# A four-layer graph network on one core: the edge sums' weighting moved to ScalarE, the last router moved into the join, and three sets of transfers moved to GpSimd's queue

## The chip, the cores and the metric

The kernel runs on one core of a Trainium2 chip. The core has five engines, each with its own queue of instructions that it takes in order: TensorE (PE, with its weight loads, PEld), VectorE (DVE), ScalarE (ACT), GpSimd (POOL) and SyncE (SP). SP, ACT and POOL also issue transfers (DMAs); a transfer stands in the queue of the engine that issues it, so an issue that has to wait holds whatever stands behind it. The metric is the time of one execution on the device, in microseconds (us). Lower is better.

## The reference

3125 nodes with 256 features each go through four layers. Each layer adds a graph part (gnn) and a mixing part (mix) computed from the normalized features, and then a feed-forward part (ffn):

```python
xn = _layernorm(x, axis=-1)
x = x + _L3_gnn_ref(xn, edge_index, ...) + _L3_mix_ref(xn[None], ...)[0]
x = x + _L3_ffn_ref(_layernorm(x, axis=-1)[None], ...)[0]
```

The graph parts of layers 1, 2 and 3 are attention over edges: for every head, an edge from s to t gets `exp(leaky_relu(s_src[s] + s_tgt[t]))`, these are normalized over the edges that end in t, and the projected features of s are summed with them. Layers 1 and 2 have two such steps each (several heads, then one head of 256), layer 3 one, which it joins with a sequence part through a gate. The ffn of layers 1 and 3 sends tokens to 8 experts. Layer 1 uses the two best experts of a token and a shared one; layer 3 the best one, with places for 489 tokens per expert:

```python
probs = jax.nn.softmax(x @ gate_w + gate_b, axis=-1)
idx = jnp.argmax(probs, axis=-1)
pos = (jnp.cumsum(one_hot, axis=0) * one_hot).sum(-1).astype(jnp.int32) - 1
kept = pos < C
buf = jnp.zeros((E, C, D)).at[idx, pos_safe].set(x, mode='drop')
hmid = jax.nn.relu(jnp.einsum('ecd,edf->ecf', buf, w1) + b1[:, None, :])
ybuf = jnp.einsum('ecf,efd->ecd', hmid, w2) + b2[:, None, :]
y_tok = ybuf[idx, pos_g] * (prb * kept)[:, None]
```

## The kernel before

The nodes lie in 25 tiles of 125 (NT, P), held in SBUF as X. Stages that go tile by tile take them in seven groups of four tiles (GROUPS, the last has one). The layers follow each other: layer 0 to about 1497 us of the span, layer 1 to 3400, layer 2 to 4660, layer 3 to the end. The code is written in a framework that orders the instructions of each engine itself, within the blocks between branches, by an estimate of when each could run; so steps of neighbouring program parts interleave, and the order on an engine is fixed at build time. An instruction waits for semaphores of the engines and transfers that it depends on, also for the memory of a pool that is reused.

**Edge sums.** `gat_products` (L1168) sums over edges as dense products. For each head the exponential of the leaky sum is split in a factor of the source (`gpre`, L1180), one of the target (`mine`) and a maximum. `h` holds the projected features of all tiles with a column of ones. It is multiplied by `gpre` in place, tile by tile (L1187 to L1189), every third tile on POOL, the others on DVE. Then, for five groups of five target tiles, the factors of the targets are spread into rows (PE product L189, copied by ACT and DVE in turn, L78 and L80), and for each of the 25 source tiles s an adjacency block `a` is loaded by SP, DVE makes the weights t from it (L1232), and PE adds t times h (L1237). With narrow heads `sums_by_feature` (L1252) does the same the other way round, for four columns of 7, 6, 6 and 6 target tiles, with t on DVE in L1308 and the products in L1313 and L1322. The function is used five times: layer 1's four heads of 128 (from 1657 us) and one of 256 (2332), layer 2's four of 64 (3630) and one of 256 (4160), and layer 3's four of 64 (5522). `shares` (L1336) and `elu` (L1383) finish each target tile through the function `use` that the caller gives.

**Second weights.** `gat_heads` (L1392) loads W2 and forms its products with the two attention vectors (`folded`, L973 and L974 on DVE) after the first projection of the layer is done, in its own pool.

**Layer 1's experts.** In `l1_ffn` 50 scatters on POOL's queue (`scatter`, L2272) write every token twice into rows in DRAM, sorted by expert; the last four columns of a row tell which token it is and its weights. These columns are loaded back as `ends` (L1580) by ACT's queue, in two halves of 112 and 13 partitions (L886 and L887 in `halves`). Ten steps on DVE (L1585 to L1594) make from them where each result goes. Meanwhile PE runs the shared expert group by group: eight hidden blocks, each with its gelu on ACT (L605), then four output tiles that DVE adds to X (L1604). The results wait in PSUM banks of a pool of seven. In DVE's order the ten steps stand after the additions of the first group and ahead of all others.

**Layer 3.** The normalized features are in DRAM. `l3_gnn` loads them as `local` on ACT's queue (L2319). `l3_local` (L2012) adds the bias to them on POOL (L2037) and runs the edge sums; its `use` adds the sums to `local` and takes the elu. `l3_join` (L2430) gathers the sequence part's rows (`gather`, L2268), normalizes both, computes a gate and a feed-forward part, adds the result z to X on POOL (L2500), normalizes X into `wide` and turns it into XNT for PE. `l3_ffn` (L2520) then fills two DRAM buffers with zeros (buf, where the experts' tokens go, and ybuf, where the results go; L2540 and L2543, by SP and ACT in turn), computes the router's logits for all tiles on PE, the softmax, each token's rank over experts, its position, and its place `put` (L2586), sends 25 scatters on POOL's queue to buf, and runs the experts one after the other: SP loads weights and rows `xr` (L2606), PE turns the rows, hidden, output; the results are scattered to ybuf.

Of the kernel before, what the change touches and what calls it, by code (L numbers as in the profile page):

```python
# [11 lines left out]
F32 = mybir.dt.float32  # L12
# [48 lines left out]
class Net:  # L61
# [1106 lines left out]
    def gat_products(self, far, h, al, heads, width, loops, use):  # L1168
# [3 lines left out]
        with ExitStack() as es:  # L1172
# [14 lines left out]
            for s in range(NT):  # L1187
                eng = nc.gpsimd if s % 3 == 2 else nc.vector
                eng.tensor_mul(h[:, s], h[:, s], pre[:, s, :, None].to_broadcast([P, heads, width + 1]))  # L1189
            if width < 96:  # L1190
                self.sums_by_feature(es, mine, over, h, heads, width, loops, use)
                return
# [20 lines left out]
            for g in range(NG):  # L1213
# [10 lines left out]
                for s in range(NT):  # L1224
                    a = ap.tile([P, GW], F32, name="a")
                    self.load_edges(a, self.adj_rows(), s, g)
                    if loops and s // GB == g:
                        blk = a[:, (s % GB) * P:(s % GB + 1) * P]
                        nc.vector.tensor_add(blk, blk, self.ident[:P, :P])
                    t = tp.tile([P, heads, GW], F32, name="t")  # L1230
# [21 lines left out]
    def sums_by_feature(self, es, mine, over, h, heads, width, loops, use):  # L1252
# [35 lines left out]
        for i0, n in COLUMNS:  # L1288
# [10 lines left out]
            for s in range(NT):  # L1299
                a = ap.tile([P, most], F32, name="a")  # L1300
                self.halves(nc.sync, a[:, :w], self.adj_rows()[s * P:(s + 1) * P, i0 * P:i0 * P + w])
                if loops and i0 <= s < i0 + n:
                    blk = a[:, (s - i0) * P:(s - i0 + 1) * P]
                    nc.vector.tensor_add(blk, blk, self.ident[:P, :P])
                t = []
# [86 lines left out]
    def gat_heads(self, prefix, h, al, h2, al2, heads, width, loops, eps):  # L1392
# [4 lines left out]
        h2v = h2[:, :, 0, :D]  # L1397
        with ExitStack() as es:
            wp = es.enter_context(self.pool("tg_w"))
            kp = es.enter_context(self.pool("tg_k", 2))  # L1400
            w2 = wp.tile([128, chunks, D + 2], F32, name="w2a")
            nc.sync.dma_start(w2[:, :, :D], self.ins[prefix + "W2"].rearrange("(c p) m -> p c m", p=128))
            b1 = self.rows(wp, prefix + "b1")
            with self.pool("tg_f") as fp:
                self.folded(fp, w2[:, :, :D], chunks, 1, [prefix + "a_src2", prefix + "a_dst2"],
                            w2[:, :, D:])
# [125 lines left out]
    def l1_ffn(self, given):  # L1532
# [8 lines left out]
        with ExitStack() as es:  # L1541
# [10 lines left out]
            with ExitStack() as es2:  # L1552
# [27 lines left out]
                self.halves(nc.scalar, ends, rows[:, D:].rearrange("(q p) c -> p q c", p=P))  # L1580
# [154 lines left out]
    def layer1(self):  # L1735
# [4 lines left out]
        with self.pool("g1_h2") as low:  # L1740
            last = self.last_terms(low)
            with self.pool("g1_h") as hp:
                with self.pool("in1") as ip:
# [3 lines left out]
                self.gat_heads(pre, h, al, *last, 4, 128, False, 1e-16)  # L1747
# [189 lines left out]
    def layer2(self):  # L1937
        pre = "L2_gnn_"
        with self.pool("g2_h2") as low:
            last = self.last_terms(low)  # L1940
            with self.pool("g2_h") as hp:
                with self.pool("in2") as ip:
# [3 lines left out]
                self.gat_heads(pre, h, al, *last, 4, 64, True, 0.0)  # L1946
# [68 lines left out]
    def l3_local(self, out, h, al, far, flag, most, found):  # L2015
# [4 lines left out]
        with ExitStack() as es:  # L2020
# [16 lines left out]
            nc.gpsimd.tensor_add(out, out, gb[:, None, :].to_broadcast([P, NT, D]))  # L2037

            def use(pp, i, acc, eps):
                x = kp.tile([P, D], F32, name="agg")  # L2040
                self.shares(kp, x, acc, 4, 64, less[:, i, :] if eps is None else eps)
                nc.vector.tensor_add(out[:, i, :], out[:, i, :], x)
# [232 lines left out]
    def l3_gnn(self):  # L2275
# [5 lines left out]
        with self.pool("in3_k") as keep:  # L2281
# [32 lines left out]
            with self.pool("in3_t") as tp:  # L2314
                xnt = tp.tile([128, KC, N], F32, name="XNT")
                wide = h.rearrange("p i h c -> p i (h c)")
                with self.pool("g3_h") as hp:
                    local = hp.tile([P, NT, D], F32, name="local")
                    self.halves(nc.scalar, local, rows.rearrange(by_tile, p=P))  # L2319
                    self.l3_local(local, h, al, *found)  # L2320
                    lp = over.enter_context(self.pool("out_ps", 3, PSUM))
                    self.l3_join(rows, local, self.order, ys, wide, xnt, lp)
                self.l3_ffn(wide, xnt, lp)
# [106 lines left out]
    def l3_join(self, rows, local, rank, ys, wide, xnt, lp):  # L2430
# [5 lines left out]
        with ExitStack() as es:  # L2436
# [6 lines left out]
            b2, fg = (self.rows(sp, pre + k) for k in ("ff2_b", "ln2_g"))  # L2443

# [64 lines left out]
            gated(*GROUPS[0], *turned[0])  # L2509
            for k, group in enumerate(GROUPS):  # L2510
                if k + 2 <= last:
                    got[k + 2] = fetched(*GROUPS[k + 2])
                if k + 1 <= last:
                    gated(*GROUPS[k + 1], *turned[k + 1])
                joined(*group, turned[k][0])
                if k + 2 <= last:
                    turned[k + 2] = halves_of(*GROUPS[k + 2], *got[k + 2])

    def l3_ffn(self, wide, xnt, lp):


# [191 lines left out]
```

## Time and profile before

| what | us |
|---|---|
| median of 3 runs | 6647.1 (6640.66 to 6662.06) |
| the profiled execution | 6652.58 |
| its span in the trace | 6650.5 |
| PE busy in it | 5730.2 |
| layer 3 from the first edge-sum product to the first expert | 5531 to 6368 |

The profiled execution's mean granted clock of TensorE is 0.911 of full speed. A row of the timeline gives the start in us from the span's start, the duration, the engine, the line of the code, the operation, output and inputs with shapes, and how many such instructions are taken together (x17). Brackets at its end give how long the engine had been idle before and what it was released by; ACTq and SPq are the queues that issue transfers. In a table of groups the columns are busy time, mean duration of one in ns, and idle time before it. Idle time of an engine matters where another engine waits for it.

### The profile page before, as it was taken

Reading aid. Unit: us, or ns where it says so; the run is one execution under the profiler, and the core shown is the slowest. Engines: PE = TensorE matmul, PEld = TensorE weight load, DVE = VectorE, ACT = ScalarE, POOL = GpSimd, SP = SyncE. Lnnn points to the kernel's source line nnn. Section 1 sums busy time; section 2 is a strip of 40 time slices with the busy share of each in tenths; the row PEclk is TensorE's granted clock in tenths of the full one; section 3 lists DMA queues with packets and bytes.
Section 4 is the critical chain, followed back from the end, with each engine's and each line's share of the span. In section 5 each row is a group of like instructions: output and inputs, shape, how many; then the busy total and the mean of one; then the engine's idle time right before and its main releaser. Section 6 shows DMA issues by size and latency. Waiting matters only on the chain. (4 is left out here: it accounts for less than half of the span.)

```text
span 6650.5 us, 80016 instructions
## 1 busy us (share of the span) xinstructions
PE 5730.2 (86%) x30063; PEld 3902.5 (59%) x30063; DVE 3734.0 (56%) x7804; ACT 1695.3 (25%) x3532; POOL 917.8 (14%) x714
## 2 busy tenths in 40 slices
PE   5887999996999998699976999999878887997876
PEld 4555975664899877468853344776534443333644
DVE  7734333128877644115036887546378888886433
ACT  2433432331011100113333011002256560003411
POOL 0000100004000012301111000120334552002021
PEclk7888999997999999789987999999889998998888
DMA  2644668101222143215520222430332223222132
GB/s 80 106 64 67 181 197 244 31 5 68 62 63 63 45 140 111 66 51 168 173 88 20 83 81 61 138 112 1 88 46 57 57 50 94 71 77 69 46 120 94
DMA packets 436886, 571.69 MB, mean 86 GB/s; under 512 B 130447, under 2 KB 321372, under 8 KB 432687
## 3 DMA queue, kind: packets, MB, share of 16 engines
q1 hardware_dynamic: 363116, 468.81, 26.4%
q10 hardware_dynamic: 44907, 68.00, 3.7%
q0 software_dynamic: 28416, 29.15, 1.6%
q8 instruction: 252, 4.13, 0.3%
q14 instruction: 195, 1.59, 0.1%
HBM read 450.03 MB, written 115.55 MB: 85 GB/s over the span
## 5 line engine op out<-in xcount | busy, mean ns | idle before, releaser
L1232 DVE SCALAR_TENSOR_TENSOR t<-rows,over,a 125x625 f32<-125x625 f32 x750 | 619.6, 866 | 426.3 <-PE acc L1237 418.9
L1308 DVE SCALAR_TENSOR_TENSOR t<-rows,over,a 125x750 f32<-125x750 f32 (+1 forms) x800 | 793.3, 1045 | 75.4 <-PE acc L1322 70.6
L1313 PE MATMUL acc<-t,g_h 125*64 125x375 f32 (+1 forms) x3200 | 596.5, 500 | 12.2 <-DVE t L1308 12.2
L1237 PE MATMUL acc<-g_h,t 125*125 125x129 f32 x5000 | 574.5, 274 | 6.2 <-ACT x L1363 3.5
L1237 PE MATMUL acc<-h,t 125*125 125x257 f32 x2500 | 558.4, 383 | 19.8 <-DVE t L1232 10.0
L1237 PEld LDWEIGHTS acc<-g_h,t 125*125 125x125 f32 x5000 | 566.2, 188 | 10.8 <-ACT x L1363 4.2
L1237 PEld LDWEIGHTS acc<-h,t 125*125 125x125 f32 x2500 | 467.3, 189 | 103.9 <-PE acc L1237 18.8
L1313 PEld LDWEIGHTS acc<-t,g_h 125*64 125x64 f32 x3200 | 220.0, 136 | 340.1 <-issue 238.8
L1322 PE MATMUL acc<-t,g_h 125*32 125x375 f32 (+1 forms) x3200 | 359.1, 496 | 0.0
L2215 POOL TENSOR_TENSOR bx<-h,crow 128x500 f32<-128x500 f32 (+1 forms) x224 | 263.7, 1195 | 308.9 <-issue 79.3
L2221 PE MATMUL y<-bx,ident 128*128 128x500 f32 (+1 forms) x448 | 222.7, 611 | 66.0 <-POOL bx L2215 64.3
L931 DVE SCALAR_TENSOR_TENSOR X<-ps_out,prob,X 125x256 f32<-125x256 f32 x200 | 87.9, 479 | 338.7 <-PE ps_out L181 338.5
L2212 DVE TENSOR_TENSOR_SCAN h<-da,state,bx 128x500 f32<-128x500 f32 (+1 forms) x224 | 246.2, 1130 | 18.3 <-ACT da L2210 15.8
L605 ACT ACTIVATE h<-ps_hidden,L_ffn_b,bn_s 128x500 f32<-128x500 f32 (+1 forms) x224 | 160.4, 723 | 350.9 <-PE ps_hidden L181 330.1
L1322 PEld LDWEIGHTS acc<-t,g_h 125*32 125x32 f32 x3200 | 99.6, 109 | 236.3 <-issue 235.5
L181 PE MATMUL ps_hidden<-xbt,w 128*128 128x250 f32 x928 | 206.2, 380 | 22.3 <-ACT xbt L166 21.9
L864 PE MATMUL agg<-h,few 125*125 125x257 bf16 x1875 | 212.6, 274 | 4.3 <-ACT few L861 2.2
L864 PEld LDWEIGHTS <-few 125*125 125x125 bf16 x1875 | 207.9, 137 | 6.1 <-ACT few L861 3.3
L181 PE MATMUL ps_out<-w,hb 128*125 128x256 f32 x928 | 205.0, 379 | 0.0
L181 PEld LDWEIGHTS ps_hidden<-xbt,w 128*128 128x128 f32 x928 | 175.1, 191 | 49.0 <-ACT xbt L166 28.6
L181 PE MATMUL ps_hidden<-XNT,L_ffn_W 128*128 128x500 f32 (+1 forms) x448 | 195.8, 562 | 0.0
L181 PEld LDWEIGHTS ps_out<-w,hb 128*125 128x125 f32 x928 | 174.0, 188 | 25.9
(765 smaller groups left out, 9461.0 us busy)
## 6 DMA issues: line engine op xcount, KB each, us to landing
a<-adj SPq DMA_DIRECT2D x500, 273.4 KB
a<-adj SPq DMA_DIRECT2D x150, 328.1 KB
arow<-adj SPq DMA_DIRECT2D x25, 1367.2 KB
adj<-block SPq DMA_DIRECT2D x22, 1531.2 KB
w<-in_L_ffn_W1p SPq DMA_DIRECT2D x29, 1024.0 KB
w<-in_L_ffn_W2p SPq DMA_DIRECT2D x29, 1024.0 KB
crow<-crows ACTq DMA_DIRECT2D x96, 250.0 KB
a<-adj SPq DMA_DIRECT2D x50, 382.8 KB
```

Of the source, the lines that this page charges most:

```text
L181: self.nc.tensor.matmul(ps, lhsT[k], rhs[k], start=(k == 0), stop=(k == n - 1))
L605: self.nc.scalar.activation(out[:, f, :], ps[:, :nt], func, **kw)
L864: nc.tensor.matmul(acc[b][:P, :D + 1], few[:, b * P:(b + 1) * P], h[k][:, s, :], start=(s == 0 and k == 0), stop=(s == NT - 1 and k == 2))
L931: nc.vector.scalar_tensor_tensor(x, ps, prob[:, g + j, e:e + 1], x, op0=ALU.mult, op1=ALU.add)
L1232: nc.vector.scalar_tensor_tensor(t[:, hd, :], rows[:, hd, :], over[:, s, hd:hd + 1], a, op0=ALU.max, op1=ALU.mult)
L1237: nc.tensor.matmul(acc(b, hd), t[:, hd, b * P:(b + 1) * P], h[:, s, hd, :], start=(s == 0 and first), stop=(s == NT - 1), skip_group_check ...
L1308: nc.vector.scalar_tensor_tensor(t[hd][:, :w], rows[hd][:, :w], over[:, s, hd:hd + 1], a[:, :w], op0=ALU.max, op1=ALU.mult)
L1313: nc.tensor.matmul(acc[k][c][q * width:(q + 1) * width, :c1 - c0], h[:, s, 2 * k + q, :width], t[2 * k + q][:, c0:c1], start=(s == 0), sto ...
L1322: nc.tensor.matmul(acc[pairs][c][hd * 32:(hd + 1) * 32, :c1 - c0], h[:, s1, hd, width:].to_broadcast([P, 32]), t1[hd][:, c0:c1], start=(s1 ...
L2212: nc.vector.tensor_tensor_scan(h[:, :w], da[:, :w], bx[:, :w], state[:, c, s:s + 1], op0=ALU.mult, op1=ALU.add)
L2215: nc.gpsimd.tensor_mul(bx[:, :w], h[:, :w], crow[:, :w])
L2221: nc.tensor.matmul(acc[c][:, :w], self.ident, terms[c][:, :w], start=(s == 0), stop=(s == S - 1))
```

## The change

1. **Weighting.** The loop over all tiles ahead of the edge sums is gone. A function `weigh(s)` multiplies one tile by its factors on ACT, one instruction per head, and is called for each source tile in the first group (or first column).
2. **Second weights.** A new function `last_weights` loads W2 and folds it; layers 1 and 2 call it before the layer's input is formed.
3. **Layer 1's columns.** `ends` is loaded by POOL's queue.
4. **Layer 3's local part.** `local` is loaded by POOL's queue. The bias is added to each tile's sums on DVE in `use`, no longer to all of `local` on POOL.
5. **Zeros.** A new function `l3_buffers` fills buf and ybuf by POOL's queue, in 8 and 7 transfers, before `l3_local`.
6. **Router.** A new function `l3_router` is set up in `l3_join`. Logits of a group are computed in the join one group later. Positions are settled in two stretches, tiles 0 to 15 and 16 to 24, each with its own softmax and with counts carried over in `before`; the choice is made by the largest probability and the first expert among equals, without ranks. The first stretch's steps are written into the join after its fifth group, the second's after its end; each sends its scatters.

```diff
-            for s in range(NT):
-                eng = nc.gpsimd if s % 3 == 2 else nc.vector
-                eng.tensor_mul(h[:, s], h[:, s], pre[:, s, :, None].to_broadcast([P, heads, width + 1]))
+            def weigh(s):
+                for hd in range(heads):
+                    nc.scalar.activation(h[:, s, hd, :], h[:, s, hd, :], AF.Copy, scale=pre[:, s, hd:hd + 1])
...
+                    if g == 0:
+                        weigh(s)
                     t = tp.tile([P, heads, GW], F32, name="t")
...
+                if i0 == 0:
+                    weigh(s)
                 t = []
...
+    def last_weights(self, pool, prefix, wide):
+        chunks = wide // 128
+        w2 = pool.tile([128, chunks, D + 2], F32, name="w2a")
+        self.nc.sync.dma_start(w2[:, :, :D], self.ins[prefix + "W2"].rearrange("(c p) m -> p c m", p=128))
+        b1 = self.rows(pool, prefix + "b1")
+        with self.pool("tg_f") as fp:
+            self.folded(fp, w2[:, :, :D], chunks, 1, [prefix + "a_src2", prefix + "a_dst2"], w2[:, :, D:])
+        return w2, b1
...
-                self.halves(nc.scalar, ends, rows[:, D:].rearrange("(q p) c -> p q c", p=P))
+                self.halves(nc.gpsimd, ends, rows[:, D:].rearrange("(q p) c -> p q c", p=P))
...
             with self.pool("g1_h") as hp:
+                weights = self.last_weights(hp, pre, 512)
                 with self.pool("in1") as ip:
...
-            nc.gpsimd.tensor_add(out, out, gb[:, None, :].to_broadcast([P, NT, D]))
-
             def use(pp, i, acc, eps):
                 x = kp.tile([P, D], F32, name="agg")
                 self.shares(kp, x, acc, 4, 64, less[:, i, :] if eps is None else eps)
+                nc.vector.tensor_add(x, x, gb)
                 nc.vector.tensor_add(out[:, i, :], out[:, i, :], x)
...
-                    self.halves(nc.scalar, local, rows.rearrange(by_tile, p=P))
+                    self.halves(nc.gpsimd, local, rows.rearrange(by_tile, p=P))
+                    buf, ybuf = self.l3_buffers(hp)
...
+            most = GROUPS[4][0]
+            sent = settle(0, most)
             for k, group in enumerate(GROUPS):
...
+                if k:
+                    logits(*GROUPS[k - 1])
+                if k > 4:
+                    next(sent, None)
                 joined(*group, turned[k][0])
+                if k == 4:
+                    next(sent)
...
+            logits(*GROUPS[last])
+            self.through(settle(most, NT))
...
+    def l3_buffers(self, pool):
+        zero = pool.tile([P, 4 * (D + 2)], F32, name="zero")
+        nc.vector.memset(zero, 0.0)
+        zv = buf[:32 * P, :].rearrange("(b p r) d -> b p (r d)", b=8, p=P)
+        for b in range(8):
+            nc.gpsimd.dma_start(zv[b], zero)
...
+        def logits(g, n):
+            ps = lp.tile([128, 512], F32, name="ps_router", tag="mm")
+            for j in range(n):
+                self.product(ps[:P, j * 8:(j + 1) * 8],
...
+        def settle(t0, t1):
...
+            nc.vector.tensor_sub(p, p, each(m))
+            nc.scalar.activation(p, p, AF.Exp)
...
+            yield
...
+            for i in range(n):
+                nc.vector.tensor_copy(off[:, i, :], before)
+                nc.vector.tensor_add(before, before, ps[:P, 256 + i * 8:256 + (i + 1) * 8])
...
+            for i in range(t0, t1):
+                stores.append(self.scatter(buf, put[:, i:i + 1], wide[:, i, :D + 2]))
```

## The prediction

> **What bounds it now.** I read the page first, then the waits of TensorE (PE), then the timeline around each edit.
>
> ```profile
> PE 5730.2 (86%) x30063; PEld 3902.5 (59%) x30063; DVE 3734.0 (56%) x7804; ACT 1695.3 (25%) x3532; POOL 917.8 (14%) x714
> ```
>
> PE is busy for 5730 of 6650.5 us, so the kernel is a row of PE stages with some 920 us of gaps, and an edit is worth the gap that it closes. Most edits aim at one. The first is the start of an edge-sum stage:
>
> ```profile
> 1657.58 17.19 DVE L1189 TENSOR_TENSOR g_h<-g_h,gpre 125x516 f32<-125x516 f32 x17 [0.79 <-ACT gpre L1180]
> ...
> 1675.16 0.99 PE L189 MATMUL ps_spread<-ident,mine 125*125 125x125 f32 x3 [14.94 <-DVE rows L78]
> ```
>
> A bracket gives the idle time before an instruction and what ended it. Seventeen multiplications fill VectorE (DVE) and PE's copies queue behind them: 14.94 us of nothing on PE. The second gap is in layer 1's expert stage, where ScalarE's (ACT) queue holds a load that waits for the scatters:
>
> ```profile
> 2772.18 3.71 ACTq L887 DMA_DIRECT2D ends<-f_rows  x1
> ...
> 2776.67 13.34 PE L181 MATMUL ps_out<-w,hs 128*125 128x256 f32 x52 [49.86 <-ACT hs L605]
> ...
> 2778.63 0.27 DVE L1585 TENSOR_TENSOR other<-ends,number 125x64 f32<-125x64 f32 x1 [67.03 <-DMA ends<-f_rows]
> ```
>
> Two engines stand there: PE 49.86 us for ACT, and DVE 67.03 us for the columns. The third is the start of layer 3's edge sums, with three gaps in a row (ACT's queue, DVE's weighting, GpSimd's weighting behind its addition):
>
> ```profile
> 5510.70 10.18 ACTq L887 DMA_DIRECT2D local<-xn  x1
> ...
> 5522.19 5.86 DVE L1189 TENSOR_TENSOR g_h<-g_h,gpre 125x260 f32<-125x260 f32 x17 [9.87 <-ACT gpre L1180]
> ...
> 5534.40 13.67 POOL L2037 TENSOR_TENSOR local<-local,L_gnn_gat_b 125x6400 f32<-125x6400 f32 x1 [30.70 <-SPq L2709]
> ...
> 5549.05 3.87 PE L1313 MATMUL acc<-t,g_h 125*64 125x500 f32 x8 [11.13 <-DVE t L1308]
> ```
>
> The last is the way from layer 3's join to its first expert:
>
> ```profile
> 6275.39 16.96 PE L181 MATMUL ps_router<-L_ffn_gate_w,XNT 128*125 128x8 f32 x80 [0.52 <-DVE z L2497]
> ...
> 6282.09 0.72 POOL L2500 TENSOR_TENSOR X<-X,z 125x256 f32<-125x256 f32 x1 [7.61 <-DVE z L2499]
> 6320.67 1.23 POOL L2272 DMA_INDIRECT buf<-g_h,put  x1 [37.86 <-DVE put L2586]
> ...
> 6356.57 1.19 POOL L2272 DMA_INDIRECT buf<-g_h,put  x1 [0.30 <-issue]
> ...
> 6368.11 2.81 PE L181 MATMUL ps_hidden<-xt,L_ffn_w 128*128 128x489 f32 x3 [0.51 <-ACT xt L80]
> ```
>
> 25 scatters at 1.494 us each, all after the last router step, all on the chain of waits.
>
> **Weighting in the first group (four places).** 17 multiplications on DVE and 8 on GpSimd (POOL) go; ACT does each tile when the group reaches it, 100 multiplications (25 with one head). ACT 125x128 with a scale is 0.359 us (the x<-acc group), 125x100 is 0.29, 125x256 is 0.49. In the changed order ACT puts 21 such between the four heads' row copies in layer 1: 21 x 0.36 + 4 x 0.47 = 9.4 us, and the heads' pipeline starts about 14.5 us earlier (first product near 1661.7, not 1676.1). After that a tile costs ACT 1.5 us and PE about 4.4, so it is hidden; at 0.5 each it still would be. The other gaps are 6.11, 6.04 and 5.96 us (2343, 3640 and 4170); I take 5.5, 6 and 5.5, what is late next being the first adjacency block (PE waits for it at 2336.5). Sum **-31.5**, bounds -15 (half) and -37 (every gap plus 4 us of second heads).
>
> **Layer 3's local part.** ACT's hold (10.18), DVE's block (5.86) and PE's hole (11.13) go, 27.2 at most. In their place: gpre near 5511.9, then 18 weightings of 0.27 and four copies of 0.58 = 7.2, then a tile of 1.1: steady products from 5521. Before, they are steady from 5549.05 with 5.6 us done earlier, as if from 5543.4. That is 22. From 5560 to 6040 PE is busy all the time, so a shift at the start reaches the end. The bias, one POOL addition of 13.67, becomes 25 DVE additions of 0.42; 19 hide under PE, the last column's 6 stand at the end: +2.5. `local` and the zero fills go on POOL's queue; nothing else of this stage is there, and their first user is some 100 us later. Sum **-19.5** (-10 to -25).
>
> **Layer 1's columns.** With `ends` on POOL's queue ACT goes on, but DVE's order is as before: the chain on `ends` stands ahead of 21 additions that free PSUM. So PE gets the rest of group 1's outputs (13.34) and three hidden blocks of 1.68, then all seven banks are taken: 18.4 us won. It then waits for `ends` as before plus some 2.6 us for the chain. ACT's queue delivers 6.8 us after the scatters end (2771.8 to 2778.6); at that speed the edit gives -14. The price on POOL's queue is not in this trace: only indirect transfers run there.
>
> ```profile
> L2272 POOL DMA_INDIRECT f_rows<-XN,put x50 | 59.5, 1190 | 51.0 <-DVE XN L1722 36.1 <-issue 14.9
> ...
> L2268 POOL DMA_INDIRECT pk_own<-tgt_parts,pk_col x1 | 0.9, 894 | 77.8 <-DVE pk_col L2386 77.8
> ```
>
> 125 rows cost 1190 ns, 16 rows 894 (the mean is the second number): 2.7 ns a row. The 114-row forms of the ybuf scatter take 1116, which makes 6.6 a row up to 125. `ends` is 125 x 64 = 8000 pieces of 16 bytes: 8000 x 2.7 = 22 us, or 53. With e us of writing and 2.5 of landing the sum is e - 18.2: -14 at ACT's speed, +4 at 22, +35 at 53. I take 24 us, next to the slope with the longer base: **+6**, bounds -14 and +35.
>
> The Trainium skill, "DMA: Bandwidth & Descriptors", "Anatomy of one DMA — SWDGE (gpsimd) path", fits a transfer from this queue as 2.0 us + bytes/436e3; for 128 KB that is an estimate of 2.3 us, and the forecast would be near 6553. Its fit has no term for pieces, and the 6.8 us here on the other path is already three times that.
>
> **W2 and its folds ahead of layers 1 and 2.** Won: PE's 11.53 us for ext at 1651.5, of which 5.27 was the load and 5.4 sixteen folding steps; I take -11. Paid: the changed order puts the same sixteen steps (5.4) between layer 0's last addition (1497.5) and layer 1's first normalization, where PE waits for DVE. In layer 2 eight steps and the load stand behind the last expert addition and ahead of all normalizations, of which the first now runs at 3428 in gaps; the load is issued about 3433 behind the last expert rows: +7 (3 to 10). Sum **+1.5** (-6 to +8). Layer 0's own reordering: 0, give or take 3.
>
> **Router and tokens.** In the changed order POOL still holds all 25 scatters behind the last addition of z (6282.09 to 6282.8), so the stretches don't start inside the join; what goes is the wait from there to 6320.67. First positions: the zero fill's hold on ACT (7.66 us before g_h) delays DVE's chain by 4.5, gone: -4.2. 80 router steps of 0.21 at clock 0.50 become 0.11 at the join's 0.93 to 1.00: 8.6 us into a PE that is busy 21 to 25 of 25: +8. Three more table loads of 1.28 on ACT and some 45 DVE steps of 0.17 in half-idle engines: +3. First scatter at 6282.8 - 4.2 + 8 + 3 = 6289.6, last 24 x 1.494 later, 6325.5: 31 earlier. The second stretch's positions (9 tiles: 18 counting steps instead of ranks and 24) are ready near 6307, before the sixteenth scatter ends at 6313.5. Paid: the first expert's weights were loaded at 6320 beside the scatters; now their memory is the join's, which the scatters read until they land, so 2 MB go ahead of the token rows on SP's queue: +5 (3 to 8). Sum **-26** (-35 to -14).
>
> On the scatters' pace, the trace has one gather of 2.17 us at 6068 against 1.21, with DVE busy 20 of 25 us there. The Trainium skill's "SBUF — State Buffer", "SBUF: two separate sides", says that DVE steps in a two-port mode keep GpSimd from writing descriptors; if it struck all of the first sixteen, 16 x 0.96 = 15 us would be an estimate of the loss, and the sum 15 higher.
>
> **The sum.** -31.5 - 19.5 + 6 + 1.5 - 26 = -69.5 on the profiled execution (span 6650.5 to 6581, with 2.1 around it). That execution took 6652.6, 5.5 above the median 6647.1; the difference taken from the median gives **6577.5**.
>
> **Rivals.**
> 1. POOL writes plain pieces about as fast as ACT's queue: -14 for +6, so 6557.5. For: the writing need not be per piece; against: the slope in rows.
> 2. The tokens' gain is lost, in a join that grows by the router and a weight load that comes late: 0 for -26, so 6603.5. For: PE is near full there; against: 37.86 us of wait on POOL.
> 3. ACT's multiplications do not keep up or come late, and the four starts gain nothing: 6609. For: they stand ahead of row copies; against: ACT is 25% busy.
> 4. **Slower than before:** POOL's writing of `ends` decides. All else is worth -75.5, and e - 18.2 passes that at e = 94 us, 11.7 ns a piece, under twice the steeper slope. At 15 ns (120 us) it is +102: 6673.5. For: DVE, and with it PE, waits for all 8000; against: both slopes are below 7 ns.
>
> Chances: forecast 0.55, rivals 0.17, 0.12, 0.08, 0.08. The range takes in 1 to 3 and most of the unknown price: 6543 to 6622. A difference under 0.3% (20 us) can't be told from none: faster 0.84 (forecast and rivals 1 to 3, less their upper tails), within 0.07, slower 0.09.
>
> **What would show it.** Right: no 14.94 and no 6 us gaps at four starts, with rows of ACT in the first group; products near 5521; PE with 18 us more before it stands in layer 1's expert stage, for `ends`, with DVE's first step about 20 us later; the first scatter near 6290 less what was won earlier, and 25 without a break. Wrong: a transfer of `ends` of more than 60 us; a break between the sixteenth and seventeenth scatter; PE waiting for ACT's g_h in a first group.

## The result and the profile after

The change made the kernel faster. On the chip of the first comparison the median is 6561.4 us (four runs, 6559.23 to 6565.17) against 6645.0 (6640.66 to 6662.06): a ratio of 0.987, 95% interval 0.9852 to 0.9888, or 83.6 us. The kernel after ran again on two other chips in the course of the experiments: there it gained 79 us (as a kernel with the same order of instructions on every engine) and 70 us (unaltered). The forecast of 69.5 us lies just under the lowest of the three.

The profiled execution has a span of 6557.4 us (clock 0.918), 93.1 less than before. The first line of its page:

```profile
PE 5712.9 (87%) x30067; PEld 3887.1 (59%) x30067; DVE 3679.8 (56%) x7761; ACT 1801.7 (27%) x3890; POOL 877.1 (13%) x695
```

PE has 17 us less to do and 93 less span: gaps closed. ACT has 106 us more, the weighting. Where they closed is read by taking the same instruction in both traces and subtracting its start; the lead grows where something was won:

| instruction | before | after | lead, us |
|---|---|---|---|
| layer 0's last addition to X | 1497.54 | 1498.80 | -1.3 |
| layer 1, first sums' first product | 1676.13 | 1659.99 | 16.1 |
| layer 1, second sums' first product | 2343.42 | 2321.22 | 22.2 |
| layer 1, first product of the first expert | 2956.40 | 2923.81 | 32.6 |
| layer 2, first sums' first product | 3644.27 | 3599.61 | 44.7 |
| layer 2, second sums' first product | 4171.00 | 4118.06 | 52.9 |
| layer 3, one and the same early column product | 5571.18 | 5491.57 | 79.6 |
| layer 3, end of the columns | 6048.50 | 5986.94 | 61.6 |
| layer 3, first gather of the join | 6055.90 | 5995.89 | 60.0 |
| layer 3, first scatter of tokens | 6320.67 | 6219.83 | 100.8 |
| layer 3, first product of the first expert | 6368.11 | 6275.56 | 92.5 |

Two entries are odd: the lead falls by 18 us inside layer 3's columns, and by 8 between the first scatter and the first expert. The timeline at the starts that the prediction spoke of follows, beginning with layer 1's sums:

```profile
1656.04 0.97 ACT L1191 ACTIVATE g_h<-g_h,gpre 125x129 f32<-125x129 f32 x3
...
1659.99 1.22 PE L1241 MATMUL acc<-g_h,t 125*125 125x129 f32 x4
```

Seventeen multiplications on DVE are gone, ACT weighs a few tiles, and products begin 4 us later. Layer 1's columns:

```profile
2750.91 2.55 POOL L886 DMA_DIRECT2D ends<-f_rows  x1 [3.52 <-DMA f_rows<-XN,put]
2753.45 0.84 POOL L887 DMA_DIRECT2D ends<-f_rows  x1
2760.35 0.27 DVE L1595 TENSOR_TENSOR other<-ends,number 125x64 f32<-125x64 f32 x1 [70.12 <-DMA ends<-f_rows]
...
2763.24 3.39 PE L181 MATMUL ps_hidden<-XNT,w 128*128 128x500 f32 x4 [38.18 <-DVE X L1614]
```

GpSimd issues the 8000 pieces in 3.4 us, not 24. PE's stand is shorter (38.18 for 49.86) and has another releaser: DVE's additions to X, which queue behind the ten steps on `ends`. Layer 3's first sums:

```profile
5449.40 1.50 POOL L886 DMA_DIRECT2D local<-xn  x1 [5.78 <-DMA ys<-yo]
...
5454.19 1.29 ACT L1191 ACTIVATE g_h<-g_h,gpre 125x65 f32<-125x65 f32 x5
...
5465.26 1.93 PE L1319 MATMUL acc<-t,g_h 125*64 125x500 f32 x2 [6.15 <-DVE t L1314]
```

The three gaps in a row are gone. And the way to the first expert:

```profile
6217.46 0.74 POOL L2513 TENSOR_TENSOR X<-X,z 125x256 f32<-125x256 f32 x1 [4.84 <-DVE slot L2632]
6219.83 1.21 POOL L2283 DMA_INDIRECT buf<-g_h,put  x1 [1.63 <-issue]
...
6238.35 0.51 DVE L2635 CAST put<-slot 125x9 int32<-125x9 f32 x1
...
6255.54 1.17 POOL L2283 DMA_INDIRECT buf<-g_h,put  x1 [0.30 <-issue]
6259.65 0.91 SPq L87 DMA_DIRECT2D L_ffn_w<-in_L_ffn_w  x2
6260.60 0.58 SPq L96 DMA_DIRECT2D L_ffn_b<-in_L_ffn_b  x1
6261.35 4.35 SPq L2667 DMA_DIRECT2D xr<-buf  x4
```

The scatters start 2.4 us after the last addition to X (38.6 before). The second places (6238.35) are there before the first sixteen scatters end, so the 25 run without a break. Then the expert's weights stand on SP's queue ahead of its rows, both behind the last scatter.

### The profile page after: what moved, and what is told of

It is laid out like the page before. It is cut to its first block, busy times and chain, and to the rows that moved or that the text cites. A ratio compares the mean times of both kernels' runs of the same rounds, so it can differ in the third digit from the quotient of the medians.

```text
span 6557.4 us, 80549 instructions
## 1 busy us (share of the span) xinstructions
PE 5712.9 (87%) x30067; PEld 3887.1 (59%) x30067; DVE 3679.8 (56%) x7761; ACT 1801.7 (27%) x3890; POOL 877.1 (13%) x695
## 5 line engine op out<-in xcount | busy, mean ns | idle before, releaser
L1314 DVE SCALAR_TENSOR_TENSOR t<-rows,over,a 125x750 f32<-125x750 f32 (+1 forms) x800 | 778.0, 1025 | 75.4 <-PE acc L1328 62.6
L1241 PEld LDWEIGHTS acc<-g_h,t 125*125 125x125 f32 x5000 | 565.4, 188 | 11.2 <-ACT x L1369 4.4
L1328 PE MATMUL acc<-t,g_h 125*32 125x375 f32 (+1 forms) x3200 | 374.0, 496 | 0.0
L2223 DVE TENSOR_TENSOR_SCAN h<-da,state,bx 128x500 f32<-128x500 f32 (+1 forms) x224 | 246.2, 1130 | 14.1 <-ACT da L2221 10.7
```

Source lines behind the costliest of these rows:

```text
L1241: nc.tensor.matmul(acc(b, hd), t[:, hd, b * P:(b + 1) * P], h[:, s, hd, :], start=(s == 0 and first), stop=(s == NT - 1), skip_group_check ...
L1314: nc.vector.scalar_tensor_tensor(t[hd][:, :w], rows[hd][:, :w], over[:, s, hd:hd + 1], a[:, :w], op0=ALU.max, op1=ALU.mult)
L1328: nc.tensor.matmul(acc[pairs][c][hd * 32:(hd + 1) * 32, :c1 - c0], h[:, s1, hd, width:].to_broadcast([P, 32]), t1[hd][:, c0:c1], start=(s1 ...
L2223: nc.vector.tensor_tensor_scan(h[:, :w], da[:, :w], bx[:, :w], state[:, c, s:s + 1], op0=ALU.mult, op1=ALU.add)
```

## The experiments

Each kernel is the kernel after with one edit, unless said otherwise. Kernels of one group ran on the same chip. A control is needed, since the same program's median was 6561, 6571 and 6575 on three chips while the kernel before stayed between 6644.9 and 6650.2. Between profiles, single stages of the same order differ by up to 8 us; layer 0's last addition alone starts between 1497.6 and 1511.2, though no edit touches layer 0.

**First group. 1. The bias back on GpSimd.** My theory was that the 18 us in layer 3's columns come from the order in which PE takes the two forms of product, 64 and 32 wide; the rival was the work beside them.

```diff
+            nc.gpsimd.tensor_add(out, out, gb[:, None, :].to_broadcast([P, NT, D]))
...
-                nc.vector.tensor_add(x, x, gb)
```

> The row of biases gb is added to the local rows by one GpSimd instruction again, as before the change, and VectorE's 25 additions of 125x256 are gone; all else is as after the change. Theory: these additions changed the fixed order in which TensorE takes layer 3's two forms of column products (286 changes between the 64-wide and the 32-wide form, 270 before the change), and that order is what cost 18 us there. Then the stretch from the first 32-wide-batch product to the last column share falls from 495 us to 477, and the time from 6561 to about 6544. Rival: the columns are slower because ScalarE now weighs the tiles or because of what lies beside them; then the stretch stays at 495 and the time at 6561 (within 3).

Measured: 6560.9 (6558.57 to 6566.78), 10.1 under the bar of this chip (6571.05, from experiment 4). In the groups of instructions by shape, the columns' products of 125x375; the numbers behind the bar are busy us and mean ns. Before, after, and this kernel:

```profile
L1313 PE MATMUL acc<-t,g_h 125*64 125x375 f32 x1400 | 266.5, 488 | 0.0
L1322 PE MATMUL acc<-t,g_h 125*32 125x375 f32 x1400 | 175.9, 484 | 0.0
```

```profile
L1319 PE MATMUL acc<-t,g_h 125*64 125x375 f32 x1400 | 267.1, 488 | 0.0
L1328 PE MATMUL acc<-t,g_h 125*32 125x375 f32 x1400 | 192.8, 484 | 0.0
```

```profile
L1319 PE MATMUL acc<-t,g_h 125*64 125x375 f32 x1400 | 267.3, 488 | 0.0
L1328 PE MATMUL acc<-t,g_h 125*32 125x375 f32 x1400 | 175.1, 484 | 0.0
```

The same 1400 instructions of the same mean occupy PE 17 us longer in the kernel after, and not in this one. Several run at a time (28 of them take 2.72 us in a row), and what changed is how many stand in a row. In the traces layer 3's products stand in 270 rows of one form before, 286 after, and 270 here. Three rows of PE's timeline after show what a row of them takes:

```profile
5701.33 1.46 PE L1328 MATMUL acc<-t,g_h 125*32 125x375 f32 x14
...
5705.40 0.82 PE L1328 MATMUL acc<-t,g_h 125*32 125x375 f32 x2
5706.15 1.49 PE L1319 MATMUL acc<-t,g_h 125*64 125x375 f32 x8
```

Two take 0.82 us, and over the whole stretch after eight take 0.91 on the average, six 1.41, ten 1.46 and fourteen 1.46. The six is an average of two cases: 27 of the 29 rows of six take 1.45 us and two take 0.83. So rows of two and fourteen take 2.28 us together and rows of six and ten, as many products, 2.87. Rows of six and of ten came up more often (13 and 11 before, 29 and 27 after), rows of two and fourteen less (33 and 20, 24 and 11). The 25 additions themselves are a rival, since they are gone here too; but PE's idle time before these products is 0.0 in all three tables, and experiment 12, which lacks the additions as well, has 274 rows and 180.4 us. So the order is what cost 17 us: shown. Why some rows of six take 0.83 and most 1.45 is open. The 17 us did not all come back, for the GpSimd addition has a price of its own, at the start of the columns in this kernel:

```profile
5495.06 22.54 POOL L2049 TENSOR_TENSOR local<-local,L_gnn_gat_b 125x6400 f32<-125x6400 f32 x1
```

```profile
5506.74 11.79 DVE L1314 SCALAR_TENSOR_TENSOR t<-rows,over,a 125x875 f32<-125x875 f32 x1 [2.72 <-DMA a<-adj]
```

```profile
5518.68 5.94 PE L1319 MATMUL acc<-t,g_h 125*64 125x500 f32 x16 [8.35 <-DVE t L1314]
```

One making of t that takes 1.12 us elsewhere took 11.79; it ended 0.9 us after GpSimd's addition (5517.60), and PE stood 8.35 us for it. The kernel before has the same pair, the addition of 13.67 us at 5534.40 that the prediction shows, and:

```profile
5534.92 14.08 DVE L1308 SCALAR_TENSOR_TENSOR t<-rows,over,a 125x875 f32<-125x875 f32 x1
```

The Trainium skill, "SBUF — State Buffer", "Who interferes with whom", has this rule: a VectorE instruction with two inputs in SBUF contends with a GpSimd instruction that reads SBUF, for a pair of ports that is an exclusive lock. The traces agree: t has two such inputs, and it stood 13.0 and 10.7 us beyond its 1.12. In experiment 1 the addition was held first: it grew by 8.87 us, and VectorE's row of t went on for 8.96 us after its start.

**2. The old weighting.** The loop ahead of the sums again; `weigh` does nothing.

```diff
+            for s in range(NT):
+                eng = nc.gpsimd if s % 3 == 2 else nc.vector
+                eng.tensor_mul(h[:, s], h[:, s], pre[:, s, :, None].to_broadcast([P, heads, width + 1]))
             def weigh(s):
-                for hd in range(heads):
-                    nc.scalar.activation(h[:, s, hd, :], h[:, s, hd, :], AF.Copy, scale=pre[:, s, hd:hd + 1])
+                pass
```

> The 25 tiles of h are weighed in one loop by VectorE and GpSimd ahead of the products again, as before the change, in all layers; all else is as after. Theory: ScalarE's weighing tile by tile gained 36.7 us at the first sums of four layers' attentions and some 10 to 20 at layer 3's, so about 6561 + 50 = 6611 (6600 to 6620). Rival, that the gains at these places came from the earlier start of what lies ahead of them (columns by GpSimd's queue, weights loaded early): then within 10 of 6561.

Measured: 6607.05 (6604.02 to 6609.94), 36.0 over the bar, and DVE's block is back:

```profile
1657.91 17.20 DVE L1190 TENSOR_TENSOR g_h<-g_h,gpre 125x516 f32<-125x516 f32 x17 [0.74 <-ACT gpre L1180]
```

The theory of the four places holds: by stages this kernel loses 14.7 us ahead of layer 1's first sums and 3.8, 5.1 and 8.3 ahead of the next three, 31.9 in all. The 10 to 20 that I added for layer 3 do not hold. From layer 3's sequence input (the first scatter of `xs`) to its first column product this kernel needs 836.8 us, the bar 835.0. So the weighting did not bind layer 3's start. The addition on GpSimd, which this kernel lacks too, did in part: PE stood 11.13 us for it before and 8.35 in experiment 1. The rest of the start's 19.5 us, some 8, is left to the load of `local` taken off ACT's queue, which is argued and not shown: no run put that load back alone.

**3. The columns of layer 1 on ACT's queue.**

```diff
-                self.halves(nc.gpsimd, ends, rows[:, D:].rearrange("(q p) c -> p q c", p=P))
+                self.halves(nc.scalar, ends, rows[:, D:].rearrange("(q p) c -> p q c", p=P))
```

> The load of the 8000 pieces of ends is issued on ScalarE's queue again, as before the change; all else is as after. Theory: ScalarE stands at it until the scatters have landed and cannot take the activations of the hidden blocks, so TensorE stands earlier (in group 2's first blocks and not its sixth) and about 11 us come back: 6572 (6568 to 6577). Rival: VectorE's ten steps on ends hold the X additions in either case and the queue is free: 6561 within 3.

Measured: 6575.6 (6571.50 to 6582.88), 4.6 over the bar. The stage itself, from the second sums' first product to the experts' first rows, takes 613.5 us against 603.0: 10.5, and PE stands 49.12 us for ACT there as before. In all the kernels that load `ends` by GpSimd's queue and keep the ten steps in their place this stage takes 602.1 to 603.5, so the rival falls by the stage; the medians of four runs, 4.6 apart, would not decide it.

**4. The ten steps written later.** The ten DVE steps on `ends` are moved behind the loop over the groups.

```diff
-                nc.vector.tensor_tensor(other, first, e, op=ALU.is_equal)
...
                     self.outward(pp, h, w2, 8, n, use)
+                nc.vector.tensor_tensor(other, first, e, op=ALU.is_equal)
...
```

> VectorE's ten steps on ends and the index come after the loop over the seven groups of layer 1's shared network and not ahead of it; the load stays where it is on GpSimd's queue. Theory: VectorE's X additions then no longer stand behind the load, TensorE's stand of 38 us in group 2 goes, the ten steps' 3 us come back at the end: 6561 - 35 = 6526 (6520 to 6532). Rival: the experts' first rows wait for what GpSimd's queue brings, so TensorE stands as long there: 6561 within 5.

Measured: 6571.05 (6569.38 to 6577.57), and nothing had moved: the framework put the ten steps where they had been, after the fourth addition. Every engine's order is that of the kernel after. So this run tells nothing of the theory, and serves as the bar of its group.

**Second group. 5. The bar.** 

> The kernel after the change, unaltered, as the bar for the three beside it on the same chip, since a kernel with the same order of instructions on every engine measured 6571 on one chip and the kernel after 6561 on another. Between 6558 and 6573; a part's worth is read against this run and not against 6561.

Measured: 6574.7 (6573.77 to 6581.21).

**6. The bias once, on DVE.**

```diff
-                nc.vector.tensor_add(x, x, gb)
+                if i == 0:
+                    nc.vector.tensor_add(out, out, gb[:, None, :].to_broadcast([P, NT, D]))
                 nc.vector.tensor_add(out[:, i, :], out[:, i, :], x)
```

> The row gb is added to all 25 tiles of the local rows by one VectorE instruction at the first column share, in place of 25 additions of 125x256; GpSimd is not asked. The order of the column products has 270 changes of form again (286 after). Theory: the 32-wide products of 125x375 fall from 193 us busy to 176 and nothing is lost at the layer's start, where GpSimd's addition of 22 us lay beside VectorE's making of the tiles: the bar - 17 (13 to 20). Rival: the one addition of 6400 elements, about 8 us on VectorE at the first share, stops the shares and with them the columns: the bar - 10 (as GpSimd's addition gave), or less.

Measured: 6569.4 (6565.70 to 6580.10), 5.2 under the bar, with an interval of the ratio (0.987 to 0.990) that overlaps the bar's (0.9883 to 0.9913): alone inconclusive. The trace tells more, though the profiled execution was the slowest of the four (6580.1), so that its stages don't add up to the median's gain. The 32-wide products are at 175.1 us busy again, so the order is confirmed with GpSimd out of it. But the framework set the addition ahead of all tiles, where DVE waits for the load:

```profile
5487.60 6.83 DVE L2053 TENSOR_TENSOR local<-local,L_gnn_gat_b 125x6400 f32<-125x6400 f32 x1 [20.61 <-DMA local<-xn]
```

From the sequence input to the first column product it takes 860.2 us against 832.0, from there to the end of the columns 502.0 against 523.9. Of these 28 us, 7 lie ahead of the sequence part's last result, where the edit does nothing; the rest is this wait, for which neither theory nor rival had a place. In this kernel and in the first, the join from its first gather to the first scatter is 6 to 7 us longer than the bar's, its first gate products starting some 6 us later (35.8 and 36.6 us after the first gather, the bars 29.9 and 30.2); why is open.

**7. The ten steps held back by data.** As experiment 4, and the first steps read a cell that the last addition to X writes:

```diff
+                nc.vector.tensor_copy(other[:, 0, 0:1], self.X[:, NT - 1, 0:1])
+                nc.vector.scalar_tensor_tensor(own[:, 0:1], self.X[:, NT - 1, 0:1], 0.0, own[:, 0:1],
+                                               op0=ALU.mult, op1=ALU.add)
                 nc.vector.tensor_tensor(other, first, e, op=ALU.is_equal)
```

> As the kernel with the ten steps late, but the first of them now reads a cell that the last X addition writes, so that no scheduler can set them ahead of the group loop again. Two VectorE steps of one column are new. Theory: TensorE's 38 us in group 2 and its 39 at the weight load go, and the experts start earlier: the bar - 35 (30 to 38). Rival 1: the experts' own rows come no earlier, for weights and rows are loaded by SyncE behind something else: the bar - 0 to - 10. Rival 2: TensorE without a pause gets a lower clock in the shared network and gives a part back: the bar - 25.

Measured: 6531.5 (6530.61 to 6533.66), 43.1 under the bar; the stage takes 562.3 us against 602.4. PE runs through:

```profile
2739.72 7.07 PE L181 MATMUL ps_out<-w,hs 128*125 128x256 f32 x32
2746.63 13.58 PE L181 MATMUL ps_hidden<-XNT,w 128*128 128x500 f32 x32
2760.04 10.31 PE L181 MATMUL ps_out<-w,hs 128*125 128x256 f32 x47
```

The view begins and ends inside a row of 64 products. No gap is left where there were 38 us. Neither rival shows: the experts start 40 us earlier, and the granted clock is 1.00 from 2700 to 2800. So of what the stage lost before the change, the queue that loads `ends` was worth 10.5 us (experiment 3) and the place of ten short steps in DVE's order 40.

**8. Places of the scatters in another pool.** `put` is allocated beside the turned tokens and handed to the join, not taken from the join's own pool.

```diff
+                put = tp.tile([P, NT], I32, name="put")
...
-        put = qp.tile([P, NT], I32, name="put")
```

> The 25 columns of places that the scatters read lie in the pool of the turned tokens and not in the join's own pool, which is freed for the experts' weights. Theory: the first expert's weights waited 10.1 us on SyncE's queue for the last scatter, because they land on the places it reads, and they load ahead of the expert's rows; with the places apart they load while the scatters run and TensorE's first expert product comes 13 us after the last scatter's start and not 20: the bar - 7 (5 to 9). Rival: the rows' own landing bounds the first product and the weights do not: the bar - 0 to - 2.

Measured: 6565.4 (6562.84 to 6567.02), 9.3 under the bar; from the first scatter to the first expert product 48.2 us, the bar 55.9. SP's queue in this kernel:

```profile
6251.84 0.94 SPq L87 DMA_DIRECT2D L_ffn_w<-in_L_ffn_w  x2
6252.83 1.26 SPq L96 DMA_DIRECT2D L_ffn_b<-in_L_ffn_b  x1
6272.37 1.44 SPq L2667 DMA_DIRECT2D xr<-buf  x4
```

The weights go while the scatters run (6232.7 to 6269.6) and only the rows wait. The 8 us (7.7 in this stage) were the memory of a 25-column table that the scatters read, under the weights' place.

**Third group.** It had no bar of its own; by the ratios 0.987 to 0.990 of the others to its kernel before (6650.05) it lies between 6564 and 6582. **9. The folds behind the input.**

```diff
-        with self.pool("tg_f") as fp:
-            self.folded(fp, w2[:, :, :D], chunks, 1, [prefix + "a_src2", prefix + "a_dst2"], w2[:, :, D:])
...
                     xn, xnt = self.layer_input(ip)
+                    self.fold_last(weights, pre, 512)
```

> W2 is still loaded before the layer's input, but its folds (four VectorE steps in layer 1, 5.4 us) stand behind the input's norms instead of ahead of them. Theory: VectorE's wait of 4.5 us for the load and the 5.4 of folds leave the start of layer 1: from layer 0's last X addition to the first XN 1.5 us and not 10.4, and the bar - 8 (6 to 10). Rival: layer 0's last X addition holds the norms anyway, or TensorE's first products of layer 1 wait for a slower thing: the bar within 3.

Measured: 6552.7 (6542.35 to 6556.51), 20.9 under the kernel with the old order of W2 in the same group. More than the theory allowed, and the trace says why. In the kernel after:

```profile
1503.76 0.76 DVE L973 TENSOR_TENSOR fold_t<-w2a,fold_a 128x256 f32<-128x256 f32 x2 [4.47 <-DMA w2a<-in_L_gnn_W]
...
1509.18 2.68 DVE L153 TENSOR_SCALAR XN<-X,li_mv,li_rs 125x256 f32<-125x256 f32 x8
```

With the folds behind:

```profile
1448.52 1.38 DVE L153 TENSOR_SCALAR XN<-X,li_mv,li_rs 125x256 f32<-125x256 f32 x4
...
1462.04 1.38 DVE L153 TENSOR_SCALAR XN<-X,li_mv,li_rs 125x256 f32<-125x256 f32 x4
```

DVE normalizes layer 1's groups as layer 0 finishes them, from 50 us before its end; five groups are done when layer 0's last addition comes. From that addition to the first product of the sums 138.2 us pass (after 161.2, before 178.6). The folds did not only cost their 5.4 us and the 4.5 of waiting: standing first in DVE's order, they barred every normalization.

**10. W2 as before the change.** Load and folds stand in `gat_heads` again.

> W2's load and folds of layers 1 and 2 stand behind the heads' first products again, as before the change. Theory: the step was a wash or a small loss for layer 1 (10 us lost at the start, about as many won ahead of the second sums) and a small gain in layer 2 (5 to 7): the bar + 3 (-3 to + 8). Rival: it was one of the change's real gains, 15 us or more: the bar + 15.

Measured: 6573.6, with a wide spread (6550.69 to 6581.06), inside the range of the bar. By stages: 159.7 us from layer 0's last addition to the sums (after 161.2), 664.5 to the second sums (after 661.2), 1275.1 to layer 2's sums (after 1278.4). Against the kernel after that is 1.5 less, 3.2 more and 3.3 less: a wash, as the theory had it.

**11. One stretch.** All 25 places are settled behind the last logits.

```diff
-            sent = settle(0, most)
...
-            self.through(settle(most, NT))
+            self.through(settle(0, NT))
```

> The places of all 25 tiles are settled once, behind the last group's logits, and all 25 scatters start there; the logits still come group by group. Theory: the first scatter starts 19.6 us later (6238.4 and not 6218.8 in the profile after) plus some 6 us of settling 25 tiles instead of the last ones, and nothing behind it takes that up, since 25 scatters of 1.49 us then stand between the last place and the experts: the bar + 24 (20 to 30). Rival: 16 scatters of the first stretch only move a queue that was not the bound, so the bar + 0 to + 5.

Measured: 6594.9 (6591.34 to 6598.13), 13 to 31 over the bar. The join from its first gather to the first scatter takes 250.2 us against 223.9 in the kernel after and 225.9 in experiment 10, so 24 to 26 more. All places come in one piece, and the scatters behind them:

```profile
6256.16 0.18 DVE L2630 CAST put<-slot 125x25 int32<-125x25 f32 x1
6257.25 1.20 POOL L2283 DMA_INDIRECT buf<-g_h,put  x1 [29.80 <-issue]
```

GpSimd had stood idle for 29.80 us; in the kernel after the first sixteen scatters, 23.8 us of them, fall into this time.

**12. Four edits together.** Experiments 7, 8 and 9, and the bias added once on DVE but held behind the first column share by reading it (274 rows of one form):

```diff
-                nc.vector.tensor_add(x, x, gb)
+                if i == 0:
+                    late = wp.tile([P, D], F32, name="late")
+                    nc.vector.scalar_tensor_tensor(late, x, 0.0, gb, op0=ALU.mult, op1=ALU.add)
+                    nc.vector.tensor_add(out, out, late[:, None, :].to_broadcast([P, NT, D]))
                 nc.vector.tensor_add(out[:, i, :], out[:, i, :], x)
```

> Four edits of the kernel after the change together: VectorE's ten steps on ends held behind the last X addition of layer 1's shared network (measured alone -43 against its bar), the places of the scatters in a pool of their own (-9), the folds of W2 in layers 1 and 2 behind the layer's input instead of ahead of it (not measured yet), and the row gb added once on VectorE, held by a dependence behind the first column share (274 changes of form against 286). Theory: they lie in different stages and add up: 40 + 8 + 9 + 10 = 67 off a bar of 6561 to 6575, so 6495 to 6508. Rival: the folds and gb give nothing or lose in the join's first halves what they win: 6515 to 6530.

Measured: 6497.9 (6487.31 to 6508.85), a ratio of 0.9774 (0.9758 to 0.979) to the kernel before. It is faster than both kernels, and lies within the theory's 6495 to 6508. The page:

```profile
PE 5715.2 (88%) x30067; PEld 3891.4 (60%) x30067; DVE 3672.7 (56%) x7740; ACT 1797.0 (28%) x3886; POOL 877.8 (14%) x695
```

The 32-wide products stand at 180.4 us, between the two orders, and the columns from first to last product take 510.7 us against 523.9 at the bar of the second group. The folds gave more than the theory had (21 for 9), so the other three gave some 12 less than their sum, and that the total lies in the range is partly luck. Against the profile of the kernel after, the stages of the ten steps, of the folds, of the columns and of the way to the first expert are 40, 22, 10 and 7 us shorter, but layer 1's experts are 3 us longer, the way from layer 2's second sums to layer 3's first column product 10, and the join 5. The held bias alone was not tried.

## Why the prediction was right, and where it was not

The time fell in the predicted range and on the predicted side, 16 us under the forecast on the first chip and closer on the others. Its sum was nearer than its parts, and that is luck: layer 3's columns lost 18 us that no term had, and layer 1's columns gave 10.5 where the sum had +6.

- **Weighting, -31.5: right.** Taking it back costs 36.0 (experiment 2).
- **Layer 3's local part, -19.5: the start right, the rest wrong.** The lead grows from 60.1 us at the last result of the sequence part to 79.6 at an early column product, 19.5 as forecast; then 18.0 are lost in the columns. The step that failed is "19 hide under PE, the last column's 6 stand at the end: +2.5". The additions did hide as work. What they did was to shift, at build time, the order in which PE takes two forms of product, and that cost 17 us (experiments 1, 6 and 12). I asked how long the new instructions take and not what an order computed from estimates does when 25 instructions join. The reading of the old gap was off too: I put PE's 11.13 us at 5549 to GpSimd's weighting behind its addition. It was one DVE instruction of 14.08 us, held while the addition ran.
- **Layer 1's columns, +6: wrong in size, so rival 1 came true.** The mis-sized term is GpSimd's writing. I took 2.7 ns a piece from scatters, where a row is an address read from memory, and 24 us; plain pieces cost 0.27 ns and the whole load 3.4 us. What was right is the frame: the prediction's e - 18.2 with e = 3.4, and 6.1 us from the end of issuing to DVE's first step in place of the 2.5 assumed, gives -11.2; experiment 3 says -10.5 in its stage. The constant was not worked out to the end, though: the terms written there (18.4 won, 2.6 for the chain, 2.5 of landing against 6.8) add up to e - 20.1, which would give -13.1. The Trainium skill, "DMA: Bandwidth & Descriptors", "Anatomy of one DMA — SWDGE (gpsimd) path", led to an estimate of 2.3 us from issue to landing; measured are 9.4. Its fit was nearer than my slope and still four times too short. That DVE's ten steps would hold PE whatever queue loads `ends` was said ("DVE's order is as before"); that they alone held 40 us was not drawn from it.
- **W2 and its folds, +1.5: right as a sum** (experiment 10), by smaller terms than I wrote: -3.2 and +1.5 in layer 1 instead of -11 and +5.4, +3.3 in layer 2 for +7. I saw that the folds stand "between layer 0's last addition and layer 1's first normalization" and missed that without them the normalizations would not stand there at all (experiment 9, 21 us).
- **Layer 0, 0 give or take 3: right**, -1.3, in part by luck, since layer 0 differs by 13.6 us between profiles of kernels that the edits leave alike there.
- **Router and tokens, -26: right, with larger terms.** The first scatter came 40.8 us earlier relative to the join's first gather, not 31, and the weights ahead of the rows took back 8.3, just over the upper end of "+5 (3 to 8)". Their cause, the memory that the scatters read, was named, and experiment 8 confirms it. Two stretches are worth some 24 of the 32 (experiment 11). The slowing of the scatters that the Trainium skill's "SBUF — State Buffer", "SBUF: two separate sides", made possible, 15 us, did not show: 25 scatters took 36.9 us from the first start to the last end, 1.49 from one to the next. VectorE's share beside the slow gather was also misread: from 6068 to 6093 it is busy for 17.7 us, not 20.

The parts measured sum to 36.0 + 1.5 + 10.5 - 1.6 - 1.3 + 32.5 = 77.6 us, inside the 70 to 84 of the medians; they come from medians and from stages on several chips, so they are good to several us only. The profile's 93.1 has 15 more. Some 10 of them are the choice of executions: the profiled one before is 7.6 us above its median, the one after 2.2 below. By place, 7 lie in layer 3's sequence part, which the change does not touch; stages of one and the same order differ by as much, and I give it no cause.

Open: why the join's first gates come some 6 us later when the bias leaves the columns; what the bias held behind the first share is worth alone; what the load of `local`, the zero fills and the logits inside the join are worth, each of which no run put back alone; and why the kernel after gains between 70 and 84 us from chip to chip while the kernel before does not move. In the profiles, 12.4 of the 14.7 us between the kernel after on the first chip and on the third lie in layer 0, where nothing was edited; on the second chip layer 0 is as short as on the first.

## What to carry to other kernels

Where an order is fixed at build time from estimates, ask of each added instruction what it stands ahead of, not how long it takes: ten steps of 0.2 us in front of the wrong neighbour cost 40 us here, sixteen folds cost 21, and moving the source lines did nothing until a data dependence held them. When a transfer changes its place, look at whose memory it lands on: here the last reader there set the wait. And before an engine's gap is given to the instruction next to it, look for one instruction many times its usual length: here it told of an engine that was blocked, not slow.

## What the runs showed of the hardware

- The four plain loads on GpSimd's queue in the kernel after took GpSimd about 0.6 us and 0.27 ns a piece, counted by the shapes in the code: 7168 pieces 2.55 us, 2800 pieces 1.50, 832 pieces 0.84, 325 pieces 0.71. Its plain stores do not follow this: the zero fills of ybuf, 500 pieces of 1 KB, took 1.31 to 1.39, and those of buf, 125 pieces of 4 KB, 0.52 to 0.60. From the start of issuing 8000 pieces of 16 bytes to the first use it was 9.4 us.
- Runs of 32-wide products (375 columns) between 64-wide ones do not cost by their number: in the kernel after 2 take 0.82 us, 8 take 0.91 on the average, 6 take 1.41, 10 and 14 take 1.46. Six cost half as much again as eight.
- A GpSimd addition of 125x6400 held one VectorE instruction for 13.0 us in the kernel before. Put back into the kernel after, where it began inside a row of them, the addition itself grew from 13.67 to 22.54 us and then held the next one for 10.7.
